# Four graph layers in one kernel: the last count of the second pair, the third layer's first slabs and the hooks of the first pair are put elsewhere

## The chip, the cores and the metric

The kernel runs on one core of one Trainium2 chip. The metric is the device time of one execution in microseconds (us). The kernel before the change took 2545.91 us, the median of three runs (2542.84, 2545.91 and 2551.58).

## What is computed

A graph of 3327 nodes has features x (3327 x 256) and a symmetric, weighted, sparse adjacency matrix adj (3327 x 3327). Four layers follow each other, and each adds to x what a different graph network makes of the relu of the layernorm of x:

```python
h = jnp.maximum(_layernorm(x), 0.0); x = x + adj @ (h @ W.T + b)                  # layer 0
h = jnp.maximum(_layernorm(x), 0.0); x = x + _L1_gnn_ref(h, adj, adj, ...)         # layer 1
#   filt = tanh(adj * adj) * (adj > 0), the 700 largest of each row are kept
#   relu(new_adj @ (tanh(h @ W_proj + b_proj) @ W_gcn) + b_gcn)
h = jnp.maximum(_layernorm(x), 0.0); x = x + _L2_gnn_ref(h, adj, W)                # layer 2
#   A = adj + I; d = A.sum(1) ** -0.5; relu((d * A * d) @ (h @ W.T))
h = jnp.maximum(_layernorm(x), 0.0); x = x + _L3_gnn_ref(h, adj, ...)              # layer 3
#   twice: A = top-p (0.9) of softmax(q @ k.T); Xf = R @ Xf, R = (adj + I) / row sums;
#   Xa = A @ Xa; Z += Xf @ U1[n].T + Xa @ U2[n].T; then layernorm(h + Z)
```

The kernel also counts the positive entries of each row of adj in its first passes over the matrix; the filter of layer 1 needs the number.

## The kernel before, in words

**Tiles and pairs.** The nodes lie in T = 26 tiles of 128 rows. Layers 0 to 2 take them as H = 13 pairs, tile p with tile p + 13. The product of a pair's rows of adj with the 3327 x 256 right-hand side is done in a Strassen-Winograd form: seven half-size products in place of eight. The columns are cut in three, `CUTS = ((0, 5), (5, 9), (9, 13))` (L32), and each cut of a pair has a number of steps, seven for each of its 5, 4 or 4 column blocks, 91 in a pair. A step is a fp32 matmul that the trace shows as two records. Inside a cut, `Product.steps` (L587, matmul L598) goes through the seven products in the order of `PLACE`: a11, a12, s1, a22, a21, s4, s2, where a11 to a21 are the four quads of adj and s1, s2, s4 (and a changed a21) are sums of them.

**The feed.** `Feed.load` (L518) issues four DMAs on SP's queue for the four quads of a cut (L527), and, in layers 0 and 2, the count of the positive entries on DVE. `Feed.adding` (L540) makes the sums on DVE: s1 at L549, a21 at L550, s2 at L551, s4 at L552. `Feed.upto(n)` (L559) loads two cuts ahead of cut n, adds one ahead, and stores some of the sums to DRAM (`s_dram`, L574) for layer 3. The buffers of quads are three deep, those of sums two.

**Counting.** `counter` (L698) makes bf16 sums of the positive entries of the quads (L708, L710), folds them behind the last cut (L713, L714, L715), and `done` sums them over the partitions with one matmul (pc, L720) and copies the result (L721). In layer 0, `finish0` calls `done0(p)` for the first two pairs itself (L782), so this matmul stands on PE directly behind the steps of pair 1.

**Order.** PE's order is always that of the program text. The other engines' order comes from the scheduler (program order, priorities, `issue_after`), save in the first two pairs of layer 0: `first_two_in` (L794 to L875) is run under a manual schedule for DVE, SP and ACT, so there the order is the one written: loads of x, the layernorms and turns of all 13 pairs, then products of pairs 0 and 1 side by side, cut by cut, with `add()`, `load()` and `count()` between them. In it, the count of the last cut of pair 1 (`last.pop(0)()`, L873) follows `feed.upto(5)`, which loads the third pair's cuts and makes the third pair's first sums, and `work_of(4)`.

**Hooks.** When the rows of a pair are finished, the next layer's work for it is done between the steps of the following pair: `turn` (four transposes pt on PE, L415, evicted by ACT, L419), in layer 1 also `hidden` (L471), and a last stage that ends with the right-hand side of the next layer: `second` (L486, copied by ACT at L489), `scaled` (L491), or for layer 3 `keys` (keys' matmul L268). Each is called behind a numbered step: `WHERE` (L629) by the number of stages, `WHERE_KEYS` (L630) in layer 2, `WHERE_FIRST` (L631) in pair 0 of a layer, where the steps that need the newest right-hand side count from 1000. The first cut of pair 1 is brought forward into pair 0 in layers 1 and 2 (`early`).

**Layer 3.** The R @ Xf part is again Strassen-Winograd, with slabs of 832 KB, three buffers: `PropagatedPair.load` (L1223) issues them on SP (L1228 from adj, L1230 from s_dram) and lets POOL add the identity to four of seven (L1232). Pair 0 takes its products in the order of `FIRST_PHASES`: slabs 1, 2, 3 first. Buffers being free, the scheduler issues slabs 1 and 2 of pair 0 at the start of the program. The entry into the layer (L1637 to L1670) makes the four combinations of the right-hand side (`combine`, L1205), the centre of the keys (`key_sum` L1000, `centre` L1012), the first logits (`prepare`, pl, L1039) and the first threshold search.

Of the kernel before, what the change touches and what calls it, by code (L numbers as in the profile page):

```python
# [17 lines left out]
ALU = mybir.AluOpType  # L18
# [12 lines left out]
H = T // 2  # L31
# [16 lines left out]
def kernel(  # L48
# [22 lines left out]
    nc = tc.nc  # L71
# [77 lines left out]
    def merged(*plans):  # L149
        out = {}  # L150
        for p in plans:
            for k, v in p.items():
                out.setdefault(k, []).extend(v)
        return out
# [76 lines left out]

    kq = const.tile([P, NC, 3, DA], F32, name="kq")

    def load_kq(w):
# [54 lines left out]
    def layers_0_to_2(again):  # L291
# [11 lines left out]
        tag = "b" if again else "a"  # L303
# [204 lines left out]
        class Feed:  # L508
# [9 lines left out]
            def load(self, p, c):  # L518
                a, b = CUTS[c]
                name = f"{tag}{self.layer}_{p}_{c}"  # L520
                if c == 0:
                    self.x2[p] = work.tile([P, 2, D], F32, tag="x", name=f"x_{name}", bufs=3)
                    self.load_x(p, self.x2[p])
                q = self.quads[p, c] = {}
                for i, j in QUADS:
                    s = raw.tile([P, 5, P], F32, tag=f"a{i}{j}", name=f"a{i}{j}_{name}")[:, : b - a, :]
                    self.loaded = nc.sync.dma_start(s, adj_t[p + i * H, :, j * H + a : j * H + b, :])  # L527
                    if self.change:
                        self.change(s)
                    q[i, j] = s  # L530
                if self.count:
                    if self.to_count is None:
                        self.count(p, c, q)
                    else:
                        self.to_count.append(functools.partial(self.count, p, c, q))
# [90 lines left out]

        WHERE = {2: (60, 84), 3: (50, 64, 80), 6: (12, 22, 34, 46, 58, 70)}  # L629
        WHERE_KEYS = (74, 89)  # L630
        WHERE_FIRST = {2: (58, 86), 3: (54, 72, 92)}  # L631

        def products(layer, width, rhs, feed, finish, before, pair_after, following=None, counted=None, begin=None):

            todo = before.stages if before else []
            n, early = 0, []
            for p in range(H):
                if begin and p < 2:  # L640
                    if p == 0:
                        n, firsts = begin(lambda p: Product(layer, p, rhs, feed, width))
                    prod = firsts[p]
                else:
                    prod = early[0] if early and p == 1 else Product(layer, p, rhs, feed, width)
                    if p == 0:
                        for c in range(len(CUTS) if not before else 0):
                            combine_nodes(rhs, *CUTS[c])
                        if before:
                            combine_nodes(rhs, CUTS[2][0], H - 1)  # L650
                    at = WHERE_KEYS if layer == 2 and p else (WHERE if p else WHERE_FIRST).get(len(todo), ())
                    hooks = dict(zip(at, todo))
                    if counted:
                        hooks[62] = functools.partial(counted, p)

                    def steps(prod, c, a, b, past=0):
                        for at in prod.steps(c, a, b):
                            if at + past in hooks:
                                hooks[at + past]()

                    for c, (a, b) in enumerate(CUTS):
                        if early and p == 1 and not c:
                            n += 1
                            continue
                        feed.upto(n)
                        if p == 0 and before and b == H:
                            steps(prod, c, a, b - 1)
                            early.append(Product(layer, 1, rhs, feed, width))
                            steps(early[0], 0, *CUTS[0], 12 * 7)
                            combine_nodes(rhs, b - 1, b)  # L670
                            steps(prod, c, b - 1, b, 1000)
                        else:
                            steps(prod, c, a, b)
                        n += 1
                        if p == H - 1 and c and following:
                            combine_nodes(following, *CUTS[c - 1])
                    feed.upto(n)
                y, p3 = prod.result()
                x2 = feed.x2.pop(p)
                with tc.high_priority() if p == H - 1 else nullcontext():  # L680
                    finish(p, x2, y, p3)
                    pair = pair_after(p, x2)
                todo = pair.stages if p or not begin else []
                if begin and p == 1:
                    todo = first.stages + todo
                first = pair
            return pair
# [65 lines left out]
        if not again:  # L753
# [40 lines left out]
            def first_two_in(product):  # L794
# [71 lines left out]
                count()  # L866
                count()
                run(add())
                last = feed.to_count
                feed.to_count = None  # L870
                feed.upto(5)
                work_of(4)
                last.pop(0)()  # L873
                work_of(5)
                return len(order), prods  # L875

# [97 lines left out]
    def layer_3_in(again, tag, big, ep, w3, sm3, h3, kT0, ksum0, left):  # L974
# [25 lines left out]
        def key_sum(kT, ksum, name):  # L1000
            total = sm3.tile([P, 1], F32, tag="ktotal", name=f"ktotal_{name}{tag}")

            def by_tensor():
                pk = one_bank(f"pk_mean_{name}{tag}")
                nc.tensor.matmul(pk[:, :1], halves, total, start=True, stop=True)
                return pk

            with tc.high_priority():
                nc.vector.tensor_reduce(total, ksum, AX.X, ALU.add)
            return by_tensor  # L1010
# [176 lines left out]
        def propagated_steps(acc, step, m, xf):  # L1187
# [3 lines left out]
            for n, k in enumerate(order):  # L1191
# [6 lines left out]
                nc.tensor.matmul(acc[:, :D], slab[g][:, j, :], xf[:, k, :], start=(n == 0), stop=(n == T - 1))  # L1198
                yield n

        PHASES = (1, 2, 5, 4), (6, 7, 3)
        FIRST_PHASES = (1, 2, 3), (5, 7, 6, 4)
        PLACE3 = {2: (0, 0), 1: (0, 1), 4: (0, 2), 5: (0, 3), 6: (1, 0), 7: (1, 1), 3: (1, 2)}

        def combine(h, ts, a, b):  # L1205
            def part(i, j):
                return h[:, i * H + a : i * H + b, j * P : (j + 1) * P]

            t1, t2, t3, t4 = (ts[:, n, a:b, :] for n in range(4))
            nc.vector.tensor_tensor(t1, part(0, 1), part(0, 0), ALU.subtract)  # L1210
            nc.vector.tensor_tensor(t3, part(1, 1), part(0, 1), ALU.subtract)
            nc.vector.tensor_tensor(t2, part(1, 1), t1, ALU.subtract)
            nc.vector.tensor_tensor(t4, part(1, 0), t2, ALU.subtract)

        class PropagatedPair:

# [4 lines left out]
                self.last = step == 1 and p == H - 1  # L1221

            def load(self, n):  # L1223
                p = self.p
                x = self.slabs[n] = slabs.tile([P, H, P], F32, tag="slab", name=f"slab3{tag}_{self.step}_{p}_{n}")
                if n in (1, 2, 4):
                    i, j = {1: (0, 0), 2: (0, 1), 4: (1, 1)}[n]
                    self.loaded = nc.sync.dma_start(x, adj_t[p + i * H, :, j * H : (j + 1) * H, :])  # L1228
                else:
                    self.loaded = nc.sync.dma_start(x, s_dram[:, p, {5: 0, 6: 1, 7: 2, 3: 3}[n]])  # L1230
                if n in (1, 4, 5, 7):
                    nc.gpsimd.tensor_tensor(x[:, p, :], x[:, p, :], ident, ALU.add)  # L1232

            def right(self, n, k):
                if n in (1, 2, 3):
# [316 lines left out]
        with tc.manual_schedule(engines=PE_ALONE):  # L1552
# [82 lines left out]
                    return accs[0]  # L1635

            with tc.issue_after(left.made.ins):  # L1637
                combine(h3, ts, 0, H)
            for i in range(EARLY):
                plan = {}  # L1640
                if props:
                    p = props.pop(0)
                    plan = {6: [lambda: p.scale(last_exp)], 13: [p.turn], 20: [p.sums]}
                if i == 0:
                    left.pool, left.bank = (w3, "eT", 3), one_bank
                    propagate_first(0, dict(zip((23, 25.4), ([what] for what in left.stages))))
                    with tc.issue_after(last_key[-1].ins):
                        constants()
                    mean0 = key_sum(kT0, ksum0, "0")
                elif i == 1:  # L1650
                    steps = prepare(0, 0, kT0)
                    centred = {6: [lambda: centre(kT0, mean0(), "0")]}
                    propagate_first(1, merged(centred, whole_run(steps, 12), plan))
                    run(find(0, 0, st0))
                    kT1, ksum1 = new_keys(f"1{tag}", big)
                else:
                    propagate_first(i, merged(whole_run(prepare(0, i - 1, kT0), 3), plan))
                    finder = find(0, i - 1, st0)
                    if i + 1 < EARLY:
                        run(finder)  # L1660
# [246 lines left out]
```

## Time and profile before

| what | value |
|---|---|
| median of three runs | 2545.91 us |
| the profiled execution's own time | 2546.84 us |
| its span in the trace | 2545.0 us |
| mean granted TensorE clock | 0.993 |
| busy: PE / PEld / DVE / ACT / POOL | 98% / 89% / 82% / 43% / 12% |
| DMA | 388.28 MB, 153 GB/s in the mean |

The profiled execution's own time is the span and 1.84 us around it. PE is TensorE's matmul stream and PEld its weight loads beside it; DVE is the vector engine, ACT the scalar engine, POOL GpSimd, SP the engine that issues most DMAs. In the lists below, "idle before, releaser" is the time that an engine stood still ahead of an instruction and the engine and line whose end let it go on. PEclk is the clock that TensorE was granted, as a share of full speed.

The span runs in this order: layer 0 to about 373 us, layer 1 to about 675 us, layer 2 to about 968 us, layer 3 to the end.

### The profile page before, as it was taken

What the parts mean: (1) busy time and instruction counts of PE and PEld (TensorE: products, weight loads), DVE (VectorE), ACT (ScalarE), POOL (GpSimd) and SP (SyncE); (2) the same over time, 40 slices, a digit from 0 to 9 for tenths busy, and PEclk for the clock granted to TensorE, in tenths of its full rate; (3) what the DMA queues carried; (4) which work ended last, traced back from release to release, by engine and by line L of the source; (5) the groups of instructions that cost most, each with busy time, mean ns of one, the idle gap of its engine ahead of it and who ended that gap; (6) DMA issues with size and microseconds to landing.
All of it is one profiled execution on the core that took longest, in us unless ns stands there. A gap on an engine that the chain in (4) does not pass through costs nothing.

```text
span 2545.0 us, 47783 instructions
## 1 busy us (share of the span) xinstructions
PE 2495.4 (98%) x17953; PEld 2259.6 (89%) x17953; DVE 2094.8 (82%) x5534; ACT 1084.7 (43%) x2158; POOL 298.6 (12%) x463
## 2 busy tenths in 40 slices
PE   9899999999999999999999999999999999999998
PEld 8899998999999998888888888888788888888887
DVE  6677688888877887788888797974899999999995
ACT  3001123434101115565656565662655565565551
POOL 2000010000000001100000000000021222222221
PEclk9999999999999999999999999999999999999999
DMA  6577765555688876323132323132424334344333
GB/s 211 175 239 230 236 212 154 162 182 176 210 297 281 272 260 197 118 94 96 63 106 82 108 82 107 64 108 101 168 93 141 107 120 134 107 125 136 126 112 108
DMA packets 181773, 388.28 MB, mean 153 GB/s; under 512 B 19741, under 2 KB 78746, under 8 KB 181530
## 3 DMA queue, kind: packets, MB, share of 16 engines
q1 hardware_dynamic: 153210, 364.31, 44.5%
q10 hardware_dynamic: 28320, 20.80, 2.5%
q8 instruction: 143, 2.34, 0.4%
q14 instruction: 100, 0.82, 0.1%
HBM read 315.44 MB, written 67.89 MB: 151 GB/s over the span
## 4 chain that ended last, share of the span: by engine, by line
PE 58%; ACT 2%; issue 0%; DVE 0%; DMA 0%; POOL 0%; POOLq 0%; ACTq 0%; DVEq 0%
PE a L213 23%; PE f1a L1263 10%; PE f0a L1263 9%; PE pl_a L1039 6%; PE pt_a L202 6%; PE u L1347 2%; PE u L1317 2%; PE f L1198 1%; ACT junk_a L1102 1%; ACT junk_a L1097 0%; ACT e_a L1064 0%; PE pkq L268 0%; DMA x_dram<-x_a 0%; PE pt_a L162 0%; PE pt_f L162 0%
## 5 line engine op out<-in xcount | busy, mean ns | idle before, releaser
L205 ACT COPY eT_a<-pt_a 128x512 f32<-128x512 f32 (+1 forms) x364 | 196.3, 555 | 375.1 <-PE pt_a L202 373.9
L213 PE MATMUL a<-h3a,eT_a 128*128 128x256 f32 x1352 | 324.1, 381 | 1.7 <-ACT eT_a L205 1.7
L213 PE MATMUL a<-vs,eT_a 128*128 128x256 f32 x1352 | 320.3, 381 | 1.3 <-ACT eT_a L205 1.3
L1126 DVE MAX8 cand_a<-w 128x8 f32<-128x128 f32 x1352 | 288.0, 278 | 4.3
L213 PEld LDWEIGHTS a<-h3a,eT_a 128*128 128x128 f32 x1352 | 244.0, 189 | 35.7 <-ACT eT_a L205 3.4
L213 PEld LDWEIGHTS a<-vs,eT_a 128*128 128x128 f32 x1352 | 244.8, 190 | 31.6 <-ACT eT_a L205 2.0
L598 PE MATMUL acc_a<-tsa,s_a 128*128 128x128 f32 (+1 forms) x2028 | 270.3, 275 | 0.0
L598 PE MATMUL acc_a<-rhs,a_a 128*128 128x128 f32 (+1 forms) x2028 | 253.4, 278 | 1.3 <-ACT rhs L489 1.3
L598 PE MATMUL acc_a<-tsa,a_a 128*128 128x128 f32 x2028 | 249.4, 275 | 0.0
L598 PEld LDWEIGHTS acc_a<-tsa,s_a 128*128 128x128 f32 x2028 | 248.6, 192 | 0.1
L598 PEld LDWEIGHTS acc_a<-rhs,a_a 128*128 128x128 f32 x2028 | 241.1, 194 | 2.9 <-ACT rhs L489 1.9
L598 PEld LDWEIGHTS acc_a<-tsa,a_a 128*128 128x128 f32 x2028 | 238.7, 192 | 0.6
L1122 DVE SCALAR_TENSOR_TENSOR w<-e_a,t_a 128x896 f32<-128x896 f32 x208 | 225.4, 1084 | 3.0
L1232 POOL TENSOR_TENSOR slab3a<-slab3a,ident 128x128 f32<-128x128 f32 x100 | 114.0, 1140 | 891.1 <-DMA slab3a<-in_adj_t_dram 335.2
L1064 ACT ACTIVATE e_a<-pl_a 128x1024 f32<-128x1024 f32 x260 | 184.5, 727 | 43.9 <-PE pl_a L1039 38.3
L202 PE MATMUL pt_a<-ident,e_a 128*128 128x128 f32 x1352 | 198.7, 273 | 0.2
L1113 DVE SCALAR_TENSOR_TENSOR w<-e_a,t_a 128x3328 uint8<-128x3328 f32 x52 | 191.6, 3684 | 4.3
L1142 DVE SCALAR_TENSOR_TENSOR e_a<-e_a,all_least 128x3328 f32<-128x3328 f32 x52 | 192.6, 3703 | 1.8
L202 PEld LDWEIGHTS pt_a<-ident,e_a 128*128 128x128 f32 x1352 | 165.4, 141 | 29.4 <-ACT eT_a L205 2.6
L419 ACT ACTIVATE xT_a<-pt_a 128x512 f32<-128x512 f32 x52 | 30.8, 593 | 347.7 <-PE pt_a L415 226.2
L738 ACT ACTIVATE a_a<-a_a 128x640 f32<-128x640 f32 (+1 forms) x156 | 101.3, 665 | 170.4 <-DVE a_a L736 152.9
L1263 PE MATMUL f0a<-tsa,slab3a 128*128 128x128 f32 x1352 | 166.0, 276 | 1.5 <-POOL slab3a L1232 1.5
(256 smaller groups left out, 4221.3 us busy)
## 6 DMA issues: line engine op xcount, KB each, us to landing
slab3a<-s_dram SPq DMA_DIRECT2D x100, 832.0 KB, 4.5
a_a<-in_adj_t_dram SPq DMA_DIRECT2D x312, 256.0 KB, 4.2
slab3a<-in_adj_t_dram SPq DMA_DIRECT2D x79, 832.0 KB, 4.6
a_a<-in_adj_t_dram SPq DMA_DIRECT2D x156, 320.0 KB, 4.0
s_dram<-s_a SPq DMA_DIRECT2D x78, 256.0 KB, 4.9
s_dram<-s_a SPq DMA_DIRECT2D x39, 320.0 KB, 4.4
x_dram<-x_a ACTq DMA_DIRECT2D x39, 256.0 KB, 3.4
s_dram<-a_a SPq DMA_DIRECT2D x26, 256.0 KB, 5.4
```

Of the source, the lines that this page charges most:

```text
L202: nc.tensor.transpose(pt[:, j, :], e[:, k * P : (k + 1) * P], ident)
L205: last_turned.append(nc.scalar.copy(eT[:, : len(blocks), :], pt[:, : len(blocks), :]))
L213: nc.tensor.matmul(acc[:, :width], ready[g][:, j, :], rhs[:, k, :], start=(k == 0), stop=(k == T - 1))
L598: nc.tensor.matmul(self.acc[:, g, at : at + wide], quads[n][:, k - CUTS[c][0], :], t, start=(k == 0 and n in (1, 4)), stop=(k == H - 1 and ...
L1039: nc.tensor.matmul(parts[h], q[h * DA : (h + 1) * DA, :], kT[h * DA : (h + 1) * DA, a:b], start=True, stop=True,)
L1064: last_exp.append(nc.scalar.activation(dst, src, AF.Exp, accum_out=parts[:, c : c + 1]))
L1113: nc.vector.scalar_tensor_tensor(junk, e, t, e, ALU.is_lt, ALU.mult, accum_out=got)
L1122: nc.vector.scalar_tensor_tensor(w[:, : (b - a) * P], eg, t, eg, ALU.is_lt, ALU.mult, accum_out=below[:, g : g + 1])
L1126: nc.vector.max(cand[:, 8 * k : 8 * k + 8], w[:, (k - a) * P : (k - a + 1) * P])
L1142: nc.vector.scalar_tensor_tensor(e, e, least, e, ALU.is_ge, ALU.mult, accum_out=st["kept"][:, m : m + 1])
L1232: nc.gpsimd.tensor_tensor(x[:, p, :], x[:, p, :], ident, ALU.add)
L1263: nc.tensor.matmul(self.accs[bank][:, c * P : (c + 1) * P], a, self.right(n, k), start=start, stop=last.get(bank) == (n, k), skip_group_ch ...
```

## The change

It has five parts.

1. In `first_two_in` the last count of pair 1 is called ahead of `feed.upto(5)`, so ahead of the sums of the third pair, and no longer behind `work_of(4)`.
2. The slabs of layer 3 that are asked for before layer 2's end (1 and 2 from adj, 3 from s_dram) are issued behind the loads of pair 4 in layer 2. POOL's additions of the identity to them move with them.
3. With three hooks in a pair (layer 1's three stages, called in layer 0 and at the start of layer 1) the step numbers go from (50, 64, 80) to (48, 61, 76), and in pair 0 from (54, 72, 92) to (52, 70, 89).
4. In layers 1 and 2, pair 0's turn is called behind step 86 of pair 1, and its last stage behind step 14 of pair 2. Before, both were in pair 1: at 60 and 84 in layer 1, at 74 and 89 in layer 2.
5. At the entry of layer 3 the combinations are no longer made at once: two first, one behind `key_sum`, one behind `centre`. `centre` moves from step 6 to step 4 and the first logits from step 12 to step 10 of the second half of the first products. The clearing of the second keys' buffers on POOL is put behind the last slab addition so far.

```diff
@@ -231,6 +231,7 @@
 
 
 
+    slabs_behind = []
     kq = const.tile([P, NC, 3, DA], F32, name="kq")
 
     def load_kq(w):
@@ -525,6 +526,8 @@
                 for i, j in QUADS:
                     s = raw.tile([P, 5, P], F32, tag=f"a{i}{j}", name=f"a{i}{j}_{name}")[:, : b - a, :]
                     self.loaded = nc.sync.dma_start(s, adj_t[p + i * H, :, j * H + a : j * H + b, :])
+                    if self.layer == 2 and p == 4:
+                        slabs_behind[:] = [self.loaded]
                     if self.change:
                         self.change(s)
                     q[i, j] = s
@@ -626,9 +629,9 @@
 
 
 
-        WHERE = {2: (60, 84), 3: (50, 64, 80), 6: (12, 22, 34, 46, 58, 70)}
+        WHERE = {2: (60, 84), 3: (48, 61, 76), 6: (12, 22, 34, 46, 58, 70)}
         WHERE_KEYS = (74, 89)
-        WHERE_FIRST = {2: (58, 86), 3: (54, 72, 92)}
+        WHERE_FIRST = {2: (58, 86), 3: (52, 70, 89)}
 
         def products(layer, width, rhs, feed, finish, before, pair_after, following=None, counted=None, begin=None):
 
@@ -650,6 +653,10 @@
                             combine_nodes(rhs, CUTS[2][0], H - 1)
                     at = WHERE_KEYS if layer == 2 and p else (WHERE if p else WHERE_FIRST).get(len(todo), ())
                     hooks = dict(zip(at, todo))
+                    if early and p == 1:
+                        hooks, carried = {86: todo[0]}, {14: todo[1]}
+                    elif early and p == 2:
+                        hooks.update(carried)
                     if counted:
                         hooks[62] = functools.partial(counted, p)
 
@@ -866,11 +873,10 @@
                 count()
                 count()
                 run(add())
-                last = feed.to_count
+                count()
                 feed.to_count = None
                 feed.upto(5)
                 work_of(4)
-                last.pop(0)()
                 work_of(5)
                 return len(order), prods
 
@@ -1198,19 +1204,23 @@
                 nc.tensor.matmul(acc[:, :D], slab[g][:, j, :], xf[:, k, :], start=(n == 0), stop=(n == T - 1))
                 yield n
 
+        added = []
         PHASES = (1, 2, 5, 4), (6, 7, 3)
         FIRST_PHASES = (1, 2, 3), (5, 7, 6, 4)
         PLACE3 = {2: (0, 0), 1: (0, 1), 4: (0, 2), 5: (0, 3), 6: (1, 0), 7: (1, 1), 3: (1, 2)}
 
-        def combine(h, ts, a, b):
+        def combining(h, ts, a, b):
             def part(i, j):
                 return h[:, i * H + a : i * H + b, j * P : (j + 1) * P]
 
             t1, t2, t3, t4 = (ts[:, n, a:b, :] for n in range(4))
-            nc.vector.tensor_tensor(t1, part(0, 1), part(0, 0), ALU.subtract)
-            nc.vector.tensor_tensor(t3, part(1, 1), part(0, 1), ALU.subtract)
-            nc.vector.tensor_tensor(t2, part(1, 1), t1, ALU.subtract)
-            nc.vector.tensor_tensor(t4, part(1, 0), t2, ALU.subtract)
+            yield nc.vector.tensor_tensor(t1, part(0, 1), part(0, 0), ALU.subtract)
+            yield nc.vector.tensor_tensor(t3, part(1, 1), part(0, 1), ALU.subtract)
+            yield nc.vector.tensor_tensor(t2, part(1, 1), t1, ALU.subtract)
+            yield nc.vector.tensor_tensor(t4, part(1, 0), t2, ALU.subtract)
+
+        def combine(h, ts, a, b):
+            run(combining(h, ts, a, b))
 
         class PropagatedPair:
 
@@ -1221,6 +1231,10 @@
                 self.last = step == 1 and p == H - 1
 
             def load(self, n):
+                with tc.issue_after(slabs_behind[-1].ins) if slabs_behind else nullcontext():
+                    self.load_now(n)
+
+            def load_now(self, n):
                 p = self.p
                 x = self.slabs[n] = slabs.tile([P, H, P], F32, tag="slab", name=f"slab3{tag}_{self.step}_{p}_{n}")
                 if n in (1, 2, 4):
@@ -1229,7 +1243,7 @@
                 else:
                     self.loaded = nc.sync.dma_start(x, s_dram[:, p, {5: 0, 6: 1, 7: 2, 3: 3}[n]])
                 if n in (1, 4, 5, 7):
-                    nc.gpsimd.tensor_tensor(x[:, p, :], x[:, p, :], ident, ALU.add)
+                    added.append(nc.gpsimd.tensor_tensor(x[:, p, :], x[:, p, :], ident, ALU.add))
 
             def right(self, n, k):
                 if n in (1, 2, 3):
@@ -1635,7 +1649,9 @@
                     return accs[0]
 
             with tc.issue_after(left.made.ins):
-                combine(h3, ts, 0, H)
+                sums_of_first = combining(h3, ts, 0, H)
+                next(sums_of_first)
+                next(sums_of_first)
             for i in range(EARLY):
                 plan = {}
                 if props:
@@ -1647,12 +1663,14 @@
                     with tc.issue_after(last_key[-1].ins):
                         constants()
                     mean0 = key_sum(kT0, ksum0, "0")
+                    next(sums_of_first)
                 elif i == 1:
                     steps = prepare(0, 0, kT0)
-                    centred = {6: [lambda: centre(kT0, mean0(), "0")]}
-                    propagate_first(1, merged(centred, whole_run(steps, 12), plan))
+                    centred = {4: [lambda: centre(kT0, mean0(), "0"), lambda: next(sums_of_first)]}
+                    propagate_first(1, merged(centred, whole_run(steps, 10), plan))
                     run(find(0, 0, st0))
-                    kT1, ksum1 = new_keys(f"1{tag}", big)
+                    with tc.issue_after(added[-1].ins):
+                        kT1, ksum1 = new_keys(f"1{tag}", big)
                 else:
                     propagate_first(i, merged(whole_run(prepare(0, i - 1, kT0), 3), plan))
                     finder = find(0, i - 1, st0)
```

## The prediction

> **What bounds the kernel now.** I read the page's busy times first, then PE's waits, then the timelines around the long ones.
>
> ```profile
> PE 2495.4 (98%) x17953; PEld 2259.6 (89%) x17953; DVE 2094.8 (82%) x5534; ACT 1084.7 (43%) x2158; POOL 298.6 (12%) x463
> ```
>
> PE is busy for 2495.4 of 2545.0 us. The change takes no matmul away, so only PE's gaps, and time that PE spends at a lower clock, are to be had. PE's waits (columns: engine and line waited for, us in total, times, longest):
>
> ```profile
> PE pc L720 <- DVE pos L715: 12.1, 2, 11.6
> PE pt_a L415 <- DVE xn_a L403: 9.1, 3, 4.4
> PE pt_a L415 <- DVE h3a L458: 2.6, 3, 1.5
> PE f0a L1263 <- POOL slab3a L1232: 1.5, 1, 1.5
> PE acc_a L598 <- ACT rhs L489: 1.3, 2, 0.7
> PE f0a L1263 <- ACT xf_0a L1272: 1.3, 1, 1.3
> ```
>
> Each is in a place that the change touches: the last count of pair 1 (11.6), the start of the program (4.30 of the xn_a waits) and pair 1 of layer 1 (4.45), pair 1 of layer 2, the entry of layer 3. PE's timeline at the first and the third:
>
> ```profile
> 96.25 0.19 PE L720 MATMUL pc<-ones,pos 128*128 128x1 bf16 x1 [11.63 <-DVE pos L715]
> 96.34 3.89 PE L598 MATMUL acc_a<-rhs,a_a 128*128 128x129 f32 x20
> ...
> 414.14 1.12 PE L415 MATMUL pt_a<-ident,xn_a 128*128 128x128 f32 x4 [4.45 <-DVE xn_a L403]
> 415.05 1.06 PE L598 MATMUL acc_a<-tsa,s_a 128*128 128x128 f32 x4
> 415.91 3.62 PE L598 MATMUL acc_a<-rhs,a_a 128*128 128x128 f32 x16
> ```
>
> The 20 records at 96.34 took 3.89 us; the same 20 at 42.81 took 2.40. The clock shows why, in a table of stretches (length; PE, PEld, DVE, ACT, POOL; clock; DMA, GB/s):
>
> ```profile
> 7.02:11.32 4.30, 0.00 (x2) 0.00 (x1) 2.63 (x11) 0.35 (x1) 1.28 (x3) 0.91 1.09 364
> 11.32:17.33 6.01, 5.68 (x17) 4.35 (x18) 5.13 (x23) 3.02 (x6) 4.20 (x10) 0.50 1.10 346
> 96.25:99.50 3.25, 3.25 (x16) 3.25 (x17) 2.54 (x7) 0.00 (x0) 0.67 (x1) 0.53 0.41 136
> 414.14:420.00 5.86, 5.86 (x28) 5.83 (x29) 4.02 (x7) 2.79 (x5) 0.00 (x0) 0.50 0.33 89
> ```
>
> After each gap of 4 us and more PE runs at half clock for a while: a removed gap gives back more than its length.
>
> [...] 0.50 to 0.53 above, while the 3.00 us wait at 1789 is followed by 0.80, so a wait under 3 us costs little more than itself. [...] a count whose data lie ready waits behind the third pair's sums.
>
> **The change part by part.** A step (two records) takes 0.2236 us: ten from 42.81 to 45.04. The sums are made against the profiled execution, 2546.84 us.
>
> *Last count (1).* The wait of 11.63 goes, and 3.89 - 2.40 = 1.49 of slow clock: 13.1. The count's five DVE operations (two L710 of 0.68, folds of 0.28, 0.23, 0.23, less overlap: 1.9) now stand ahead of the third pair's sums, where DVE is idle:
>
> ```profile
> 72.87 0.69 DVE L552 TENSOR_TENSOR s_a<-a_a,s_a 128x512 f32<-128x512 f32 x1
> 78.91 0.29 DVE L619 TENSOR_TENSOR u_a<-p_a,acc_a 128x128 f32<-128x128 f32 x1 [5.35 <-ACT p_a L614]
> ...
> 88.70 0.81 DVE L549 TENSOR_TENSOR s_a<-a_a,a_a 128x640 f32<-128x640 f32 x1
> ```
>
> So they are free: 1.9 in 5.35 idle; without that cover they would cost 1.9. But what is late next? PE goes through both pc at 84.65, ten steps of a11 and a12 take it to 84.65 + 10 x 0.2236 = 86.9, then it needs s1, whose L549 ends at 88.70 + 0.81 = 89.5. The count stood behind this in the old order, so its leaving doesn't bring it forward. New wait: 2.6. Net 13.1 - 2.6 = 10.5. Bounds: 13.1 (DVE gets s1 done sooner) and 5 (5.5 more of wait, if s1 slips by three us or the gap still slows the clock).
>
> *Slabs (2), at the start.* SP's first two issues were the slabs: 0.94 us of SP (0.72 to 1.66) and 1.7 MB, at the 414 GB/s of that stretch 4.1 us, ahead of x. DVE's first statistics waited for x until 8.23; they come at about 4.1. PE's warm-up block lasts until 7.02, so the first turn, at 11.32, can come at 7.02 at the earliest, up to 4.3 sooner. With no gap, the slow clock goes too: (1.12 - 0.60) x 2 on the turns and 3.66 - 1.89 on the projection: 2.8. DVE could be next: it is 5.13 busy of the 6.01 us after 11.32. But from 17 to 25 it waits four times for PE or ACT (1.24, 0.63, 0.63, 1.06), and that slack moves over: its last xn is at 35.9, three us ahead of its turn at 38.91. I take 6.0; bounds 0.9 (only the issue time) and 7.1.
>
> *Slabs (2), in layer 2.* SP issues two behind the loads of pair 4 (763.75 to 772.0), so they pass the stores at 772.42 and the load at 776.85, which is delayed by up to 1.7 MB, 4.3 us; its first use on DVE is at about 782.6, normally landed by 776 + 4: no cost. POOL's addition for slab 1 then stands ahead of r_a of pair 3 at 780.58; the slab, issued at 772, lands by about 775. The third slab passes one later load by 2 us, with two us of slack. I take 0; bounds -3 (one of these covers is gone) and +0.3.
>
> *Layer 1's pair 1 (4).* The wait of 4.45 goes, and the slow clock: 1.12 - 0.60, 1.06 - 0.61, 3.62 - 1.95, 1.46 - 1.06, together 3.04: 7.5. PE now goes on from 409.69; 2 steps of s2, then 20 of a11 to a21 bring it to s4 at 414.5, and DVE's L552 (414.33, 0.68) makes s4 by 415.0: a new wait of 0.55. The turn behind step 86 is called at 415.9, xn being ready at 414.4. The last stage at step 14 of pair 2 is 4 us later, long after the turn's ACT copy (0.6). Net 6.9; bounds 4 (pair 1's own turn at 60 of pair 2 finds a later DVE) and 7.5.
>
> *Layer 2's pair 1 (4).* DVE runs without a pause from 704.89 to 719.57 and ends with s4 (L552). Today PE waits 1.47 for the turn's h3a and then 0.23 for s4. With the turn moved PE is earlier at s4, waits 2.4 there, and does the turn (0.44) afterwards: the wait moves, and the turn's time is no longer in its shadow. -0.35 (a little of the s4 wait of 0.23 is saved); bounds -0.5 and +1.5 (DVE does s4 ahead of the turn's layernorm).
>
> *Hooks of three (3).* Two waits for rhs (L489) stand at the layer boundary, 0.54 and 0.73. Projections four steps earlier (0.9 us) remove the first; the second follows a write made right ahead of its reader. +0.4; bounds 0 and 0.9.
>
> *Layer 3's entry (5).* PE's wait of 1.54 for POOL's addition goes: the addition stands behind a clearing (974.51) which waited for a store. But DVE's chain goes on from there:
>
> ```profile
> 971.56 1.89 DVE L1210 TENSOR_TENSOR tsa<-h3a 128x1664 f32<-128x1664 f32 x1
> ...
> 977.24 0.17 DVE L1009 TENSOR_REDUCE ktotal_0a<-ksum_0a 128x1 f32<-128x26 f32 x1
> 977.35 2.03 DVE L1213 TENSOR_TENSOR tsa<-h3a,tsa 128x1664 f32<-128x1664 f32 x1
> ...
> 979.48 2.20 DVE L1019 TENSOR_SCALAR kT_0a<-kT_0a,kmean_0a 64x1664 f32<-64x1664 f32 x2
> ```
>
> Its order on DVE isn't changed, so kT is centred at 981.7 as before. PE gets to the centre and to the logits 1.5 to 2 us earlier and waits there for these (about 1.35 and 1.5), and at the end it still waits for ACT's copy at 992.27. Net 0; bounds -1 and +1.5.
>
> **The sum.** 10.5 + 6.0 + 0 + 6.9 - 0.35 + 0.4 + 0 = 23.4. 2546.84 - 23.4 = 2523.4. The median of the runs shown lies 0.93 under the profiled execution, so the median after would be about 2522.5; between the two I say 2523.
>
> **The rivals.** *A, the forecast*: 2519 to 2528, chance 0.70. *B, other waits take most of it*: PE, let go, runs into sums that DVE makes no earlier. For it: DVE has no pause from 84 to 97 and from 704 to 720. If the start gives 3, layer 0 5, layer 1 5.5 and layer 3 costs 0.5: 13, so 2534 to 2529; chance 0.18. *C, no new waits*: 7.1 + 13.1 + 7.5 + 0.9 + 1.5 = 30, 2516; against it the s1 at 89.5. Chance 0.06. *D, slower*: [...]the addition to slab 1 stands ahead of r_a of pair 3 in layer 2. Were the slab to land after 780.6, each us later would hold up pair 3's layernorm and with it PE by one us. From 780.6 + 23.4 = 804 on the gain is eaten; 31 us later (812) and over makes the kernel slower by over 0.3%, about 2555. Against it: a slab takes 4.6 us from issue to landing in the list of DMA issues, and SP's next stores there are issued within 5 us. Chance 0.03. *E, nothing happens* (the scheduler undoes the order, and the waits only change their names): 2540 to 2550, chance 0.03; against it, the order of the first two pairs is written by hand.
>
> **How the numbers follow.** About 0.3% (7.6 us) is what a measurement of this kernel can tell from no change: faster means under 2538.3, slower over 2553.5. A, B and C are faster: 0.94, of which I take off 0.04 for a B that goes further. The same: E and that remainder, 0.07. Slower: D, 0.03. The range from 2515 to 2535 holds A, B and C.
>
> **What would show it.** Right: the 11.63 at pc is gone and a wait of about 2.6 for s_a (L549) is there; the first statistics are at about 4 us and PE's clock doesn't fall in the first 20 us; no xn_a wait in layer 1, half a us at s4; in layer 2 a wait of 2.4 for s_a (L552) in place of h3a; no POOL wait at layer 3's entry, but one for DVE. Wrong: a first turn still after 9 us, a wait of over 4 us for sums at the third pair, POOL's r_a behind a slab addition in layer 2, or PE waiting more at the entry of layer 3 than the 2.8 of before.

## The result, and the profile after

The changed kernel took 2531.9 us (median of six runs, 2527.95 to 2534.66), the kernel before 2548.74 us beside it (six runs, 2542.55 to 2553.67): a ratio of 0.9935, 95% interval 0.9915 to 0.9955, so 16.8 us between the medians, and from 11 to 22 by the interval. The forecast was 2523: the direction was right, the size too large. The two profiled executions took 2546.84 and 2532.95 us, 13.9 apart, where the prediction's sum had 23.4.

PE's busy time is nearly the same (2493.5 us, now 99% of the span): only gaps and clock were to be had. PE's waits in the changed kernel (engine and line waited for, us in total, times, longest; line numbers of the changed kernel, so L552 is the sum s1 and L555 the sum s4):

```profile
PE pt_a L416 <- DVE xn_a L404: 3.5, 3, 1.9
PE pt_a L416 <- DVE h3a L459: 3.1, 2, 1.6
...
PE acc_a L601 <- DVE s_a L555: 3.0, 3, 2.4
PE acc_a L601 <- DVE s_a L552: 2.7, 1, 2.7
...
PE pk_mean_0a L1011 <- DVE ktotal_0a L1015: 1.5, 1, 1.5
...
PE f0a L1277 <- ACT xf_0a L1286: 0.7, 1, 0.7
PE pc L727 <- DVE pos L722: 0.3, 1, 0.3
```

The count's 11.6 and layer 1's 4.4 are gone; the waits forecast in their place are there almost to the tenth (2.66 for s1, 2.36 for s4 in layer 2, 0.48 for s4 in layer 1, 1.46 for ktotal). PE's timeline at the first and the third of them:

```profile
86.49 1.58 PE L601 MATMUL acc_a<-tsa,s_a 128*128 128x129 f32 x6 [2.66 <-DVE s_a L552]
...
402.95 1.16 PE L601 MATMUL acc_a<-rhs,s_a 128*128 128x128 f32 x8 [0.48 <-DVE s_a L555]
403.95 0.60 PE L416 MATMUL pt_a<-ident,xn_a 128*128 128x128 f32 x4
```

What was not forecast: h3a is still waited for, now at two later places, and two waits of over 1 us for xn_a are left at the start.

To see where time goes between two kernels I take the starts of the same turns (pt_a) on PE in both and compare the stretches between them: (a) program start to the twelfth turn of layer 0's opening; (b) from there to the turn of pair 2 in layer 0, which holds the last count; (c) the last turn before pair 1 of layer 1 to the turn of that pair's own rows; (d) the same around pair 1 of layer 2; (e) the next six pairs of layer 2. All in us, one profiled execution each:

| kernel | a | b | c | d | e |
|---|---|---|---|---|---|
| before | 36.75 | 100.69 | 56.96 | 50.91 | 132.12 |
| changed | 33.60 | 91.57 | 50.40 | 52.80 | 134.31 |
| changed, once more | 32.94 | 89.91 | 50.52 | 51.30 | 136.95 |
| count alone | 35.99 | 90.37 | 56.52 | 51.32 | 131.40 |
| slabs alone | 31.63 | 101.94 | 56.18 | 50.82 | 134.97 |
| pair 1's hooks alone | 35.68 | 101.98 | 50.16 | 51.18 | 131.13 |
| slabs in layer 1 | 34.68 | 91.40 | 50.49 | 51.89 | 130.58 |
| slabs in layer 1, once more | 34.36 | 91.49 | 50.59 | 53.30 | 131.11 |
| layer 1's hooks only | 33.54 | 91.47 | 50.44 | 53.14 | 134.27 |
| sums first | 32.94 | 90.43 | 50.98 | 51.35 | 132.93 |
| layer 2's sums early | 33.02 | 89.92 | 50.44 | 50.82 | 133.11 |
| warm start | 32.20 | 91.56 | 50.40 | 51.13 | 134.90 |
| all that helped | 31.91 | 87.00 | 50.50 | 49.45 | 131.86 |
| the same, old entry | 31.85 | 86.99 | 50.51 | 48.04 | 131.53 |

So the changed kernel gains 3.2 (a), 9.1 (b) and 6.6 (c), and gives back 1.9 (d) and 2.2 (e).

### The profile page after: what moved, and what is told of

It reads as the page before. It is cut to its first block, busy times and chain, and to the rows that moved or that the text cites. A ratio compares the mean times of both kernels' runs of the same rounds, so it can differ in the third digit from the quotient of the medians.

```text
span 2531.1 us, 47787 instructions
## 1 busy us (share of the span) xinstructions
PE 2493.5 (99%) x17953; PEld 2257.0 (89%) x17953; DVE 2093.9 (83%) x5534; ACT 1085.2 (43%) x2158; POOL 297.7 (12%) x463
## 4 chain that ended last, share of the span: by engine, by line
PE 59%; ACT 2%; DVE 1%; issue 0%; POOL 0%; POOLq 0%; DVEq 0%; ACTq 0%
PE a L213 23%; PE f1a L1277 10%; PE f0a L1277 9%; PE pl_a L1045 6%; PE pt_a L202 6%; PE u L1361 2%; PE u L1331 2%; PE f L1204 1%; ACT junk_a L1108 1%; PE pkq L269 0%; ACT junk_a L1103 0%; PE pt_a L162 0%; PE pt_f L162 0%; ACT eT_a L205 0%; ACT e_a L1070 0%
## 5 line engine op out<-in xcount | busy, mean ns | idle before, releaser
L213 PEld LDWEIGHTS a<-h3a,eT_a 128*128 128x128 f32 x1352 | 243.9, 189 | 35.7 <-ACT eT_a L205 3.4
L213 PEld LDWEIGHTS a<-vs,eT_a 128*128 128x128 f32 x1352 | 244.8, 190 | 31.6 <-ACT eT_a L205 2.0
```

The source lines that it names most:

```text
L213: nc.tensor.matmul(acc[:, :width], ready[g][:, j, :], rhs[:, k, :], start=(k == 0), stop=(k == T - 1))
```

## The experiments

The kernels from "count alone" to "warm start" were run once each, save where a number of runs is given. One run of the kernel before beside them took 2543.0 us (beside the first four) or 2545.5 us (beside the other four), and its six runs above lie 11 us apart. So a single total says little about a few us; what is read from these kernels is read from the stretches.

**Count alone** (part 1 on the kernel before): `count()` ahead of `feed.upto(5)`, nothing else.

> The kernel before with part 1 alone: the last count of pair 1 ahead of the third pair's sums. Theory: the wait of 11.63 us at the count's matmul goes, a wait of 2.6 to 2.7 us for the third pair's first sum (s_a) takes its place and lowers PE's clock for some matmuls, so that the end of layer 0 comes 8.7 us earlier, not the 10.5 us of the prediction, and the total is about 2538. Rival: the smaller gain in the changed kernel comes from the earlier start of the program (x and the adjacency loads meet differently); then the part alone gives 10 us or more.

2537.19 us, and stretch b is 10.3 us shorter. The wait of 2.66 for s1 stands exactly where it was forecast, but here PE's clock didn't fall behind it (the next 16 records of a21 took 1.95 us, as long as 16 of them ahead of the wait), so the rival's number came true, though not for the rival's reason. (That the total met the theory's 2538 is luck: the run of the kernel before beside it took 2543.0.) The last experiment shows when the clock falls.

**Slabs alone** (part 2 on the kernel before):

```diff
+                    if self.layer == 2 and p == 4:
+                        slabs_behind[:] = [self.loaded]
...
+                with tc.issue_after(slabs_behind[-1].ins) if slabs_behind else nullcontext():
+                    self.load_now(n)
```

> The kernel before with part 2 alone: layer 3's first slabs loaded behind pair 4's loads in layer 2. Theory: the start gains 3.1 us, and 1.5 to 3 us of it are lost again in pairs 5 to 7 of layer 2, because the slabs stand ahead of the quads of pair 5 on SP's queue, a count on the vector engine waits 5 us or more for them, and the turn's h3a comes late. Net 0.5 to 1.5 us, about 2545.5. Rival: the losses in layer 2 come from the moved hooks of pair 1 there; then this kernel keeps the whole 3.1 us to layer 3.

2543.57 us, no less than the kernel before beside it. Stretch a is 5.1 us shorter (the theory had 3.1), stretch e 2.9 us longer: the loss in layer 2 comes with the slabs, without the moved hooks. The rival falls. The changed kernel shows how. First SP's queue, then DVE:

```profile
766.97 0.59 SPq L1244 DMA_DIRECT2D slab3a<-s_dram  x1
767.61 2.07 SPq L528 DMA_DIRECT2D a_a<-in_adj_t_dram  x4
```

```profile
777.88 0.69 DVE L717 SCALAR_TENSOR_TENSOR pos<-a_a,pos 128x512 bf16<-128x512 f32 x1 [6.40 <-DMA a_a<-in_adj_t_dram]
...
779.10 0.28 DVE L622 TENSOR_TENSOR u_a<-p_a,acc_a 128x128 f32<-128x128 f32 x1
...
789.21 0.42 DVE L459 TENSOR_SCALAR h3a<-h3a 128x512 f32<-128x512 f32 x1
```

The third slab (832 KB) is issued right ahead of the four quads of pair 5's last cut. The count of these quads waits 6.40 us for them at the head of DVE's queue, and behind it stand the finishing operations of pair 4: the first (L622) begins at 779.10, though ACT copied its products out at 771.73, in 0.48 us. So h3a is ready only at 789.6, and PE waits 1.63 for it, and 1.43 at the next pair.

**Pair 1's hooks alone** (part 4 on the kernel before):

> The kernel before with part 4 alone: pair 0's turn behind step 86 of pair 1 and its last stage in pair 2, in layers 1 and 2. Theory: layer 1 gains 6.5 to 7 us; layer 2 loses about 2 us at pair 1, because the 2.4 us wait for s4 lowers PE's clock and the turn is no longer hidden in a wait; net 4.5 to 5 us, about 2542. Rival: a wait under 3 us doesn't lower the clock and layer 2 loses 0.35 us; net 6.5 us, about 2540.

2537.86 us. Stretch c is 6.8 us shorter and d 0.27 longer: the prediction's 6.9 and -0.35. PE waits 2.36 us for s4 in layer 2, and its clock stays up in this execution (stretch d takes 51.18, against 52.80 in the changed kernel, where the clock was 0.53 behind the same wait). The rival's number came true; its reason, that a wait under 3 us doesn't lower the clock, doesn't hold in other executions, as the last experiment shows.

**Slabs in layer 1** (on the changed kernel):

```diff
-                    if self.layer == 2 and p == 4:
+                    if (self.layer, p) == ((2, 4) if again else (1, 6)):
```

> The changed kernel, but slabs 1 and 2 are loaded behind the loads of pair 6 in layer 1, where the queues move about 170 GB/s, and not in layer 2, where they move about 280. Theory: the start's 3.1 us stay, and of the 2.4 us lost in pairs 3 to 8 of layer 2 at least 1.5 us come back, since no quad of layer 2 lands late; about 2531 in a run where the changed kernel takes 2533. Rival: layer 1's quads land late instead, the filter on the scalar engine comes late and the loss only changes its place.

2529.97 us; stretch e takes 130.58, six pairs without any wait of PE. The third slab is loaded early in layer 2, as in the kernel before. DVE waits only briefly for the last quad of the same cut, from the timeline of this kernel:

```profile
774.78 0.69 DVE L717 SCALAR_TENSOR_TENSOR pos<-a_a,pos 128x512 bf16<-128x512 f32 x1 [0.47 <-DMA a_a<-in_adj_t_dram]
```

At other cuts of layer 2 the same operation waits up to 3.40 us in this kernel, and PE doesn't notice; in the seven profiles with slabs loaded in layer 2 it waits 4.8 to 7.5 us at this cut, and PE's waits for h3a at the next two turns come to 1.9 to 3.3. Layer 1 lost nothing that shows. Timed:

> The changed kernel with slabs 1 and 2 loaded in layer 1, timed. Theory: 3 to 4 us under the changed kernel, as the trace of layer 2 says (from 14.3 to 18.0 us ahead of the kernel before at the end of it). Rival: of the order of the scatter of the runs, 0 to 1 us, since the runs' clock at the waits decides more.

2529.43 us (five runs), ratio to the kernel before 0.9929 (0.9916 to 0.9943), against 0.9943 (0.9930 to 0.9957) for the changed kernel beside it. The medians lie 4.3 us apart (the theory had 3 to 4), but the intervals overlap: the 3.7 us that the trace shows in one place (3.2 in this kernel's second profile) are about what the total can't tell.

**Layer 1's hooks only** (on the changed kernel, layer 2's pair 1 as before): `if layer == 1 and early and p == 1`.

> The changed kernel with the hooks of layer 2's pair 1 as before (turn at 74, last stage at 89), those of layer 1 as changed. Theory: in layer 2 PE waits about 1.5 us for h3a at the turn and 0.2 for s4 in place of 2.4 us for s4; pair 1 to pair 2 costs 0.3 us less than in the changed kernel where the clock stays high after the 2.4 us wait, and up to 2 us less where it falls. Rival: the move is a gain in layer 2 too, and pair 1 costs 1 us more here.

2533.67 us, and a miss for both: h3a was waited for 2.69 us, not 1.5, and the clock fell behind that wait (16 records of a21 and a22 in 3.11 us, where 1.95 is usual), so stretch d took 53.14. Why h3a came later than forecast is open. With old hooks and no fall stretch d takes 50.8 to 51.3, with moved hooks and no fall 51.1 to 51.4, and 51.9 in the one kernel that also waits 1.1 us for a count there. Part 4 costs some tenths of a us in layer 2; the rest is the clock.

**Sums first** (on the changed kernel): the third pair's first cut is loaded and summed ahead of pair 0's finishing work.

```diff
+                feed.load(2, 0)
+                feed.done[0] += 1
+                feed.done[1] += 1
+                *_, feed.added = feed.adding(2, 0)
+                count()
                 feed.to_count = None
...
+                with tc.issue_after(feed.added.ins) if begin and p == 0 else nullcontext():
+                    y, p3 = prod.result()
```

> The changed kernel, with the third pair's first cut loaded, summed and counted ahead of pair 0's finishing work on the vector engine. Theory: the 2.66 us wait for s_a at the third pair goes, since the sums fit in the 3.2 us in which the vector engine stands idle before pair 0's result; layer 0 ends 2.7 us earlier, 4 us if the clock fell in the run compared. Rival: the quads of the third pair land too late for that (their buffers come free late), the sums then block pair 0's finishing work, and the gain is under 1 us or a loss.

2531.77 us. The wait for s1 is gone, and one of about its size has its place, two steps later:

```profile
86.95 0.76 PE L416 MATMUL pt_a<-ident,xn_a 128*128 128x128 f32 x4 [3.11 <-DVE xn_a L404]
```

Pair 0's layernorm was pushed back by sums and counts (xn_a is written from 86.48 on, in the changed kernel from 81.04), and its turn was due at step 12. Stretch b took 90.43, against 89.91 in the changed kernel's execution without a fall: no gain. The rival's number came true, though the quads were not late, as it had it. DVE has hardly a pause here (from 74.59 to 97.16 two, of 0.91 and 0.90 us), and the new order only chose what PE waits for: 3.11 us for xn_a in place of 2.66 for s1. The consumer had to be moved as well.

**Layer 2's sums early** (on the changed kernel): `feed.upto(n + 1)` at the end of pair 0, and pair 0's turn and keys behind steps 8 and 24 of pair 2.

> The changed kernel; in layer 2 the sums of pair 1's last cut are made ahead of pair 0's finishing work, and pair 0's turn and keys are done behind steps 8 and 24 of pair 2. Theory: the 2.4 us wait for s4 in pair 1 goes (the vector engine makes s4 some 4 us earlier), and the turn finds its input ready: 2.3 us are gained in layer 2, 4 us if the clock fell in the run compared. Rival: the finishing work comes late in its turn, the vector engine being busy without a pause there, and PE waits 2 us or more for h3a at step 8 of pair 2.

2525.78 us, but most of the difference arose elsewhere: stretch d took 50.82, about 0.5 us under most kernels with part 4 whose clock didn't fall. The wait for s4 went, and PE waited 2.56 for h3a at the turn instead. The rival was right.

**Warm start** (on the changed kernel): `warm(17)` in place of the 12 warm-up matmuls, and `warm(8)` behind the first turn.

> The changed kernel with 5 more warm-up matmuls ahead of the first turn and 8 behind it, which fill PE's waits for x (their output is not used, the result is unchanged). Theory: x's own transfer sets the time of the first two turns (7.1 and 9.8 us), which stay; but PE's clock doesn't fall at 11 us, and the turns and projections behind it take 2.2 us less, so that the first product starts 1.5 to 2.2 us earlier. Rival: what follows the first turns is paced by the vector engine (layernorms every 1.5 us), and the start gains under 0.5 us.

2529.76 us. Stretch a took 32.20, 1.40 less than in the changed kernel: a little under the theory's bound. The first turns came at 8.32 and 10.55, behind the added matmuls (at 7.31 and 9.80, and 7.72 and 9.95, in the two later kernels with the same warm-up), and the start was still shorter. What goes with the shorter start is the clock: in these three kernels it doesn't fall there (in the changed kernel it was 0.50 from 11.52 to 14.93), and stretch a takes 31.9 to 32.2; in the seven profiles with moved slabs and the old warm-up in which it falls, 32.9 to 34.7. "Slabs alone" kept its clock without the added matmuls and took 31.63.

**All that helped** (slabs in layer 1, warm start, sums first with the six hooks of that pair at 28 to 82, layer 2's sums early with the turn at 22 and the keys at 38 of pair 2):

> All of what helped, on the changed kernel: slabs 1 and 2 loaded in layer 1, warm-up matmuls in the waits at the start, the third pair's sums of layer 0 ahead of pair 0's finishing work with the hooks of pair 2 of layer 0 behind steps 28 to 82, and in layer 2 the sums of pair 1's last cut early with pair 0's turn and keys behind steps 22 and 38 of pair 2. Theory: 3.7 us from the slabs, 1.4 to 2 from the start, 2.7 to 4 from the sums in layer 0 (the turn that took over their wait is now later), 2.4 to 4 from layer 2: 10 to 13 us under the changed kernel, about 2520. Rival: the vector engine has more to do than PE in both places, so a later turn only moves the wait once more, to the hidden stage or to the next sums, and the gain stays at 6 us.

2519.72 us (four runs), ratio 0.9894 (0.9879 to 0.9909). Behind the warm-up no wait of PE ahead of layer 3 is over 1.04 us. Stretch b is 4.6 us shorter than in the changed kernel and d 3.4 (of which 1.7 and 1.5 are falls of the clock that the changed kernel's execution had): with the turns moved behind the time at which DVE has their input, the wait in layer 0 is gone, that in layer 2 is down to 0.77, and the rival is wrong. 14.0 us under the changed kernel timed beside it (2533.71, below) and 12.2 under the 2531.9 above, where the theory had 10 to 13; the intervals of the ratios, here and below, don't overlap.

**The same, with layer 3's entry as before** (part 5 undone):

> The kernel with all that helped, but layer 3's entry (part 5) as before the change. Theory: part 5 only moved waits (POOL 1.5 us, later ACT 1.3, against DVE 1.5 and ACT 0.7), so from the last turn of layer 2 to the second phase's h3a products it takes 20.7 us as in the kernel before, against 20.9 to 21.0 with part 5; the total is the same within the scatter, 2518 to 2521. Rival: part 5 is a gain once the rest is faster, and the entry takes 22 us here.

2519.62 us, ratio 0.9910 (0.9893 to 0.9926). From the last turn to the second phase's h3a products it takes 962.44 - 941.62 = 20.82 us, against 20.87 with part 5; in the kernel before 20.66, in the changed 20.99. Part 5 is worth nothing, or costs some tenths.

**The changed kernel once more:**

> The changed kernel once more, beside the others on the same chip: about 2532, ratio to the kernel before 0.9915 to 0.9955 as in the result. Its profile shows whether the 2.66 us wait in layer 0 and the 2.36 us wait in layer 2 are followed by a lower clock again (theory: it differs from run to run, since the single-part kernels kept the clock after waits of the same length) or always in this kernel (rival).

2533.71 us (five runs), ratio 0.9943 (0.9930 to 0.9957). The wait for s1 had the same length in the two executions of the one program. What PE did behind it differs. Below are 2.5 us from the end of the wait for s1 and from the end of that for s4 in layer 2; the columns are those of the table of stretches in the prediction. The changed kernel, first execution:

```profile
86.49:88.98 2.49, 2.49 (x12) 2.49 (x13) 2.49 (x5) 0.00 (x0) 0.00 (x0) 0.52 0.49 187
700.88:703.38 2.50, 2.50 (x12) 2.50 (x13) 2.25 (x3) 0.00 (x0) 0.00 (x0) 0.53 0.90 293
```

And the second:

```profile
85.83:88.33 2.50, 2.50 (x22) 2.50 (x23) 2.50 (x5) 0.60 (x1) 0.00 (x0) 1.00 0.49 188
700.17:702.67 2.50, 2.50 (x22) 2.50 (x23) 2.24 (x3) 0.60 (x1) 0.00 (x0) 1.00 0.92 304
```

12 records at a clock of 0.52, or 22 at 1.00, behind one and the same wait of 2.66 us. That is worth 1.7 us in stretch b (91.57 against 89.91) and 1.5 in d.

The traces also show what differs: where the wait lies. In each of the two executions the measured changes of the clock lie whole multiples of 3.413 us apart. In the first they come at 4.69, 11.52, 14.93, 86.61, 90.02, 701.01 and 704.42, which is 2, 1, 21, 1, 179 and 1 times that length; in the second at 6.19, 9.61, 13.02, 787.85 and 791.26. (In the kernel before they come at 7.14, 10.55, 17.38, 89.06, 99.30, 413.33 and 420.15: 1, 2, 21, 3, 92 and 2 times.) I call the lengths of 3.413 us between these points slots; counted on from 13.02 and back from 787.85, slots of the second execution also end at 84.70 and 699.10. Here are the slots around the wait for s1, in the first execution:

```profile
83.20:86.61 3.41, 0.75 (x7) 0.56 (x6) 3.41 (x9) 0.00 (x0) 0.00 (x0) 1.00 0.25 77
86.61:90.02 3.41, 3.41 (x17) 3.41 (x18) 3.41 (x7) 0.60 (x1) 0.00 (x0) 0.50 0.68 257
```

And in the second:

```profile
81.29:84.70 3.41, 1.88 (x17) 1.69 (x16) 3.41 (x14) 0.03 (x1) 0.00 (x0) 1.00 0.44 138
84.70:88.11 3.41, 2.28 (x20) 2.29 (x21) 3.41 (x6) 0.60 (x1) 0.00 (x0) 1.00 0.30 113
```

In the first execution the whole wait lies in one slot, and in the next the clock is 0.50. In the second the wait is cut into 1.53 and 1.13 us, and the clock stays at 1.00. The same holds for s4: 2.36 us in one slot (clock 0.53 behind it), or 1.28 and 1.07 in two (1.00). In the fourteen profiles there are 21 waits of PE of 2.0 to 3.2 us between the start and layer 3. Behind ten the clock fell, and of each of these 2.04 us or more lay in one slot; of the eleven others at most 1.95 did. No kernel moved a wait against the slots on purpose, so this is read from the records and not tried. From the first to the second execution of the one program the slots lie 1.50 us later in the span (6.19 against 4.69), and the wait for s1 0.66 us earlier; so which of the two happened here wasn't the program's doing.

## Why the prediction was right and wrong

The result lies in the range of rival B (2529 to 2534, chance 0.18), not in that of A (2519 to 2528, chance 0.70), but B's sum didn't come true either. It had layer 0 at 5 and layer 1 at 5.5, which gave 9.1 and 6.6; its start of 3 is what was measured, and the loss in layer 2 stood in neither. Of the signs named for "right", one failed: the clock did fall in the first 20 us. None of the signs for "wrong" came.

- **Last count: right.** Net 10.5 was forecast. The three kernels without part 1 take 100.7 to 102.0 in stretch b, the changed kernel 91.6 and 89.9: 9 to 12. The new wait at s1 was foreseen at 2.6 and measured at 2.66.
- **Layer 1's pair 1: right.** Net 6.9; measured 6.6 (changed) and 6.8 (alone), with the s4 wait of 0.48 in place of 0.55.
- **Slabs, at the start: the mechanism right, the size wrong.** The term was 6.0. The three kernels with slabs at the start take 35.7 to 36.8 in stretch a, the eight profiles with the slabs moved and the old warm-up 31.6 to 34.7: 3.2 in the changed kernel, 1.0 to 5.1 over all pairs. The first statistics came at 2.92, sooner than the 4.1 of the forecast, but the step from there to the turn failed: it took x as landed once the slabs were out of the way. DVE now waits for x five times, 3.3 us in all:

```profile
2.92 0.43 DVE L387 BATCH_NORM_STATS2 st_a<-rhs 128x6 f32<-128x256 f32 x1 [0.98 <-DMA rhs<-in_x_dram]
...
5.03 0.43 DVE L387 BATCH_NORM_STATS2 st_a<-rhs 128x6 f32<-128x256 f32 x1 [0.94 <-DMA rhs<-in_x_dram]
...
8.74 0.43 DVE L387 BATCH_NORM_STATS2 st_a<-rhs 128x6 f32<-128x256 f32 x1 [0.52 <-DMA rhs<-in_x_dram]
```

So the second turn came at 9.81 (12.76 before), with PE idle for 1.95 us ahead of it, and the clock was at 0.50 from 11.52 to 14.93 (before from 10.55 to 17.38). Of the 2.8 us of slow clock that the term counted as gone only some 1 us went: a projection of 2.92 us in place of 1.89, a turn of 1.06 in place of 0.60 and a projection of 2.27 in place of 1.89 are 1.9 us still there. The warm start takes 1.4 us off.
- **Slabs, in layer 2: wrong.** The term was 0, "with two us of slack" for the third slab. It cost 2.9: stretch e takes 134.5 in the mean of the seven profiles with slabs loaded there (132.9 to 137.0; in two of them the clock falls as well), and 131.6 in the three kernels that have the slabs at the start (131.1 to 132.1). The bound of -3 held it. Two readings of SP's queue were off: the third slab was to pass one later load and passed the four quads of a cut, and slabs 1 and 2 go out behind the load that stands at 768.47 in the kernel before, not at 772.0, so they too pass four quads (769.87 to 771.71). And what the step left out is the count: in the changed kernel it waits 6.40 us on DVE for a late quad, and pair 4's finishing work, which is on the way to PE's next turn, comes behind it at 779.10. That the load itself isn't urgent for the products says nothing on that.
- **Layer 2's pair 1: right in itself**, -0.27 alone against -0.35, but -1.9 in the profiled pair. The sentence that failed is "a wait under 3 us costs little more than itself". It was drawn from one wait at 1789, and that one was misread. A figure of 0.80 comes out only as a mean over some 8 us behind the wait; right behind it the clock of the kernel before was at 0.50 for 3.3 us:

```profile
1788.99:1792.31 3.32, 3.32 (x16) 3.09 (x17) 3.18 (x6) 3.32 (x12) 0.10 (x1) 0.50 0.00 0
```

- **Hooks of three and layer 3's entry:** the wait of 0.54 went and that of 0.73 stayed; the entry moved its waits to DVE as forecast, and took 0.3 us more.

With a start of 3.2 for 6.0 and -2.9 for 0 the prediction's sum becomes 23.4 - 2.8 - 2.9 = 17.7, which lies beside the 16.8 of the timed runs. The profiled pair's 13.9 has two falls of the clock more (1.7 and 1.5). This sum is put together after the fact, from stretches of single profiles.

The runs also give a price for the clock behind a wait of 2 to 3 us: behind one and the same wait of 2.66 us the clock was 0.52 in one execution of the changed kernel and 1.00 in the other, 1.7 us apart in stretch b, and behind 2.04 us of idle time ("warm start") it fell as well. With ten falls behind 21 waits, a wait over 2 us in such a stream of products is to be priced, by my estimate, with about half of 1.7 us rather than none.

Stretch e in the changed kernel differs by 2.6 us between its two executions (134.31 and 136.95). In the second, PE waits 2.74 us for h3a in place of 1.63, and the clock falls behind that wait (from 787.85 to 791.26; the 16 records at 789.35 took 2.87 us, where 1.95 is usual); these two account for it. What stays open: why that wait is longer, and why a kernel's part up to layer 3 differs by some 4 us between two runs (the last two rows, 945.77 against 941.62 at the last turn; the difference grows by 0.7, 1.3 and 2.1 us in layers 0, 1 and 2, without a fall of the clock). Loads that land a little earlier or later may be the reason; no run isolates it.

## What to carry to other kernels

When a transfer is moved, look at who waits for the transfers behind it on the queue, and then at everything that stands behind that waiter on its engine: here a count that nobody needed soon waited 6.40 us, and it held up the layernorm that PE waited 1.63 us for. When a wait is removed on an engine that feeds a busier one, move the consumer too (here its turns by 14 to 16 steps); reordering the producer alone gave the wait a new name (2.66 us for s1 became 3.11 for xn_a). And price idle gaps of 2 to 3 us with the clock's fall as a risk (behind ten of 21 here); the clock behind each gap (here 0.52 or 1.00 over the next 2.5 us), or a second profile of the same kernel, tells it from an effect of the change.

## What the runs showed that I had not expected

The clock fell behind a wait as short as 2.04 us (in "warm start", 783.05 to 785.09; the 16 records at 785.59 then took 3.37 us, where 1.95 is usual), and behind one and the same wait in one execution and not in the other (0.52 or 1.00, in the same program); this alone moved a profiled time by 1.5 to 1.7 us a place. In the records it goes with where the wait lies against the slots of 3.413 us: 2.04 us or more in one slot behind the ten falls, at most 1.95 in the eleven other waits. Filling two waits of 1 to 2 us at the start with matmuls whose output is not used made the start 1.4 us shorter, though the first two turns came no earlier for it.
